# A feed-forward product as seven block products in place of eight, with its sums shared out anew over three engines

## The chip, the cores and the metric

The kernel runs on one core of one Trainium2 chip. A core has engines that run side by side, each through its own instructions in its own order: TensorE (PE in the profile; its weight loads are PEld), VectorE (DVE), ScalarE (ACT), GpSimd (POOL) and SyncE (SP, which here only issues transfers). TensorE writes only to PSUM, a memory of eight banks; VectorE and ScalarE read from there, and GpSimd works on SBUF alone in this kernel. The metric is device time in microseconds, as the median of a few executions.

## The reference

A block of a transformer on 4096 tokens of width 256, all in float32. With `xn = layernorm(x)`:

```
out = x + attn_block(xn) + experts(xn)

attn_block(xn):  x1 = layernorm(xn + attention(xn)) * gamma + beta
                 h  = gelu(x1 @ W1 + b1)            # W1: 256 x 1024
                 return x1 + h @ W2 + b2            # W2: 1024 x 256
experts(xn):     softmax over 8 experts, the best 2 of each token,
                 sum of share_k * expert_k(xn)      # hidden width 816
```

The change concerns the product `x1 @ W1` and what is added up around the feed-forward part: `x`, `x1`, `b2`, `h @ W2`, and for each token the two expert results with their shares.

## The kernel before

The kernel has three stages: normalization and routing; a long stage that interleaves the experts' products with attention, `STEPS = 32` steps and a few more; and at the end the feed-forward part. The change is in the last stage, which begins at about 850 us, and in a few lines that prepare it.

**The feed-forward stage** runs over `NG = 8` groups of `G = 512` tokens. A tile with 128 partitions holds 4 x 128 tokens (`TG = 4`) of width `D = 256`, or, turned, 2 x 128 features (`DC = 2`) by 512 tokens. For group g:

- `second_loads(g)` loads `x` into `acc` and the attention block's result into `x2`, both through SP's queue. `second_norm(g)` normalizes `x2` on ScalarE (line 1177), four instructions.
- `second_base(g)` puts `x + x1*gamma + beta + b2` into `acc` by three VectorE instructions of 128x1024 (lines 1188 to 1190).
- `turned2(g)` transposes `x2` on TensorE (line 1197) into two PSUM banks and ScalarE writes them to `x2T` with gamma and beta (line 1200).
- `hidden(g)` makes `hT`: for each of the `FC1 = 8` feature blocks f two matmuls with 512 moving columns into one bank (line 1210), then one GELU with its bias by ScalarE straight from the bank (line 1217).
- `sums_of_hidden(g)` makes four sums of `hT` quarters on VectorE (lines 1241 to 1245), which `second(g)` needs: the second product `h @ W2` is already done there in the form with seven block products in place of eight (Winograd's variant of Strassen's scheme). Its weight sums `V2` are made once by GpSimd in `sums_of_weights` (line 1235).
- `second(g)` has seven products p1, p2, p6, p5, p7, p3, p4, each eight matmuls of 128x128 into a bank of its own (line 1281). After each, VectorE adds the bank into `acc` (lines 1291, 1301, 1309). p1 is first copied by ScalarE to the tile `u` (line 1294).
- `picked(g)` gathers, by eight indirect transfers that GpSimd issues (line 1255), the two expert results of each token, and `combined(g)` adds them into `acc`, weighted with `share`, by eight VectorE instructions of 128x256 (line 1268).
- `store(g)` writes `acc` to the output through SP's queue.

**Order.** A manual schedule is in force: every engine gets its instructions in the order in which the code issues them, and none is moved before an earlier one of its own engine. The loop runs one group ahead with the hidden part: in turn g it issues `hidden(g)`, `second_base(g+1)`, `combined(g-1)`, `turned2(g+1)`, `second_norm(g+2)`, `picked(g)`, and then `second(g-1)` with the sums of `hidden(g)` between its products. So ScalarE's order in a turn is: eight GELUs, two copies of `turned2`, four of `second_norm`, the copy of `u`. VectorE's is: three of `second_base`, eight of `combined`, the adds of p1 and p2, two sums, p6 and p5, two sums, p7, p3, p4.

**Banks.** `bank()` hands out seven PSUM banks in rotation. A matmul that starts a bank waits until the reader of the use seven before is done.

Of the kernel before, what the change touches and what calls it, by code (L numbers as in the profile page):

```python
# [32 lines left out]
F32 = mybir.dt.float32  # L33
# [8 lines left out]
P = 128  # L42
# [61 lines left out]
def block_kernel(ctx: ExitStack, tc: tile.TileContext, a: dict, out: bass.AP):  # L104
# [1080 lines left out]
    def second_base(g, acc, x2):  # L1185

        scaled = accp.tile([P, TG, D], F32, tag="scaled", name=f"scaled{g}", bufs=1)
        nc.vector.tensor_tensor(acc, acc, bcast(beta_b2, TG, 1), ALU.add)
        nc.vector.tensor_tensor(scaled, x2, bcast(gamma, TG, 1), ALU.mult)
        nc.vector.tensor_tensor(acc, acc, scaled, ALU.add)  # L1190

    def turned2(g, x2):
        x2T = turns.tile([P, DC, G], F32, tag="x2T", name=f"x2T{g}")
# [8 lines left out]
            )  # L1202
        return x2T

    def hidden(g, x2T):
        hT = hf.tile([P, FC1, G], F32, tag="hf", name=f"hf{g}")
        for f in range(FC1):
            ph = bank(f"ph{g}_{f}")
            for c in range(DC):
                nc.tensor.matmul(  # L1210
                    ph,
                    W1[:, c, f * P : (f + 1) * P],
                    x2T[:, c, :],
                    start=(c == 0),
                    stop=(c == DC - 1),
                )
            nc.scalar.activation(hT[:, f, :], ph, AF.Gelu, bias=b1[:, f : f + 1])  # L1217
        return hT


# [27 lines left out]

    def picked(g):

        ys = []
        for i in range(g * TG, (g + 1) * TG):
            for k in range(2):
                y = got.tile([P, D], F32, tag="got", name=f"got{i}_{k}")
                nc.gpsimd.indirect_dma_start(  # L1255
                    out=y,
                    out_offset=None,
                    in_=done,
                    in_offset=bass.IndirectOffsetOnAxis(ap=slot[:, k, i : i + 1], axis=0),
                )  # L1260
                ys.append(y)
        return ys

    def combined(g, acc, ys):
        for n, y in enumerate(ys):
            t, k = n // 2, n % 2
            i = g * TG + t
            nc.vector.scalar_tensor_tensor(  # L1268
                acc[:, t, :], y, share[:, k, i : i + 1], acc[:, t, :], ALU.mult, ALU.add
            )  # L1270

    def second(g, acc, hT, v):

        t1, t2 = slice(0, 2), slice(2, 4)
        u = hf.tile([P, 2, P], F32, tag="u", name=f"u{g}")

        def product(n, left, right):
            pb = bank(f"s{g}_{n}").rearrange("p (t n) -> p t n", n=P)[:, 0:2]
            for t in range(2):
                for f in range(FH):  # L1280
                    nc.tensor.matmul(  # L1281
                        pb[:, t, :],
                        left[:, f, t * P : (t + 1) * P],
                        right[:, f, :],
                        start=(f == 0),
                        stop=(f == FH - 1),
                    )
            return pb

        def add(t, cols, pb):  # L1290
            nc.vector.tensor_tensor(acc[:, t, cols], pb, acc[:, t, cols], ALU.add)  # L1291

        p1 = product(1, hT[:, F_LO, 0:B], W2[:, F_LO, C1])
        nc.scalar.copy(u, p1)  # L1294
# [6 lines left out]
        nc.vector.tensor_tensor(u, p6, u, ALU.add)  # L1301
        add(t1, C2, u)
        yield
        p5 = product(5, v[:, 0], V2[:, 0])
        add(t1, C2, p5)
        add(t2, C2, p5)
        yield
        p7 = product(7, v[:, 2], V2[:, 2])
        nc.vector.tensor_tensor(u, p7, u, ALU.add)
        add(t2, C1, u)  # L1310
        add(t2, C2, u)
        yield
        p3 = product(3, v[:, 3], W2[:, F_HI, C2])
# [40 lines left out]
    for b in range(ALWAYS):  # L1354
# [56 lines left out]
        if b == STEPS:  # L1411
            att.close()
            wf = pool(ctx, "wf", right)
            accp = pool(ctx, "accp", right, bufs=4)
            V2 = wf.tile([P, 4, FC1 // 2, P], F32, tag="V2", name="V2")
            W1, W2 = matrix(wf, "W1", F1, DC), matrix(wf, "W2", D, FC1)
# [12 lines left out]
            x2s = {n: second_loads(n) for n in range(2)}  # L1429
        if b == STEPS + 1:  # L1430
            sums_of_weights()
            *_, r2 = rstd_of(mv2, root_of(mv2, NT, "b"), NT, "b")
            nc.vector.scalar_tensor_tensor(shift2, mv2[:, :, 0], -1.0, r2, ALU.mult, ALU.mult)
            nc.vector.tensor_tensor(beta_b2, beta, b2, ALU.add)
# [57 lines left out]


    x2Ts = {n: turned2(n, x2s[n][1]) for n in range(2)}

    for b in range(ALWAYS, BLOCKS):
        nc.gpsimd.memset(xs[b], 0.0)
# [15 lines left out]
    late_done.close()  # L1513
    experts_done.close()
    hf = pool(ctx, "hf", right, bufs=2)
    got = pool(ctx, "got", right, bufs=8)
    second_base(0, *x2s[0])
    last = None

# [4 lines left out]
    for g in range(NG):  # L1524
        if g + 2 < NG:
            x2s[g + 2] = second_loads(g + 2)
        hT = hidden(g, x2Ts.pop(g))
        if g + 1 < NG:
            second_base(g + 1, *x2s[g + 1])
        if g > 0:  # L1530
            acc = x2s.pop(g - 1)[0]
            combined(g - 1, acc, ys)
        if 0 < g < NG - 1:
            x2Ts[g + 1] = turned2(g + 1, x2s[g + 1][1])
        if g + 2 < NG:
# [104 lines left out]
```

## Time and profile before

| | |
|---|---|
| median of 3 runs | 1069.93 us (1069.36 to 1071.85) |
| the profiled execution's own time | 1071.19 us |
| its span | 1069.5 us |
| start of the feed-forward products in it | 850.7 us |
| one turn of the loop, groups 1 to 6 | 27.12 us |

Busy time in one turn (932.41 to 959.53 us): TensorE 27.12 us, VectorE 15.86 us, ScalarE 9.05 us, GpSimd 7.95 us; the granted TensorE clock is 1.00 there.

The profile is read as follows. A row of a group has the line, the engine, the operation, the tiles written and read, the shape and the number of instructions, and after the bar the busy time in us and the mean of one in ns. In the list in order of time, the first number is the start in us from the begin of the span, the second the duration, and brackets show how long the engine had been idle and what ended that. Each float32 matmul appears as two records. A matmul's end is modelled, so that the distance between starts, not the duration, is its cost in a row of matmuls.

### The profile page before, as it was taken

How to read it: one execution, taken by the hardware profiler on the slowest of the kernel's cores; microseconds unless marked ns; L12 is line 12 of the kernel's file. 1: busy time of each engine (PE TensorE's matmuls, PEld its weight loads, DVE VectorE, ACT ScalarE, POOL GpSimd, SP SyncE). 2: the span in 40 equal slices, each digit the busy share in tenths (PEclk: the TensorE clock that was granted, in tenths of full speed). 3: DMA queues.
4: the chain of work that ended last, by engine and by line, in shares of the span. 5: the costliest groups of instructions: out<-in, count | busy, mean ns of one | idle time of the engine just before them, and what ended most of it. 6: DMA issues, size and time to landing. Idle time of an engine off the chain costs nothing. (4 is left out here: it accounts for less than half of the span.)

```text
span 1069.5 us, 20380 instructions
## 1 busy us (share of the span) xinstructions
PE 1057.4 (99%) x7278; PEld 860.8 (80%) x7278; DVE 753.9 (70%) x1852; ACT 572.6 (54%) x1329; POOL 587.8 (55%) x706
## 2 busy tenths in 40 slices
PE   9998999999999999999999999999999999999998
PEld 6577887887888888888888888888887757777778
DVE  6666876886787687788888988888532455555546
ACT  4526556656657556756675666566455353333320
POOL 5417766676576666676877777767520053222220
PEclk9999999999999999999999999999999999999999
DMA  8225434445345344544544444345584343333111
GB/s 287 75 102 204 139 129 173 172 150 180 118 143 183 129 146 165 199 139 143 177 175 139 176 158 181 138 167 173 187 310 145 123 137 114 99 99 96 63 60 40
DMA packets 61047, 158.67 MB, mean 148 GB/s; under 512 B 6576, under 2 KB 46896, under 8 KB 56208
## 3 DMA queue, kind: packets, MB, share of 16 engines
q1 hardware_dynamic: 53632, 139.33, 37.4%
q0 software_dynamic: 6480, 17.70, 5.2%
q8 instruction: 59, 0.97, 0.4%
q10 hardware_dynamic: 832, 0.30, 0.1%
q14 instruction: 44, 0.36, 0.1%
HBM read 135.43 MB, written 21.89 MB: 147 GB/s over the span
## 5 line engine op out<-in xcount | busy, mean ns | idle before, releaser
L839 PE MATMUL gu<-xsT,wg 128*128 128x256 f32 (+1 forms) x1632 | 364.4, 370 | 0.0
L839 PEld LDWEIGHTS gu<-xsT,wg 128*128 128x128 f32 x1632 | 290.0, 191 | 46.5 <-DVE nm L1047 8.6
L1255 POOL DMA_INDIRECT got<-done,slot x64 | 64.6, 1010 | 177.0 <-DVE acc L1268 106.8
L847 ACT ACTIVATE gs<-gu,wg 128x256 f32<-128x256 f32 (+1 forms) x204 | 92.2, 452 | 120.4 <-PE gu L839 116.0
L1074 POOL TENSOR_TENSOR pr<-pr 128x256 f32<-128x256 f32 x128 | 114.2, 892 | 67.0 <-ACT pr L1062 67.0
L848 DVE SCALAR_TENSOR_TENSOR hT<-gu,wg,gs 128x256 f32<-128x256 f32 (+1 forms) x204 | 91.9, 461 | 78.7 <-ACT gs L847 77.8
L1075 POOL TENSOR_TENSOR pr<-pr,ident 128x256 f32<-128x256 f32 x128 | 132.8, 1037 | 10.0
L1062 ACT ACTIVATE pr<-pr,nm 128x256 f32<-128x256 f32 x256 | 126.8, 497 | 1.0 <-ACT xsT L831 0.6
L1210 PE MATMUL ph<-x2T,W 128*128 128x512 f32 x256 | 111.0, 592 | 0.0
L1217 ACT ACTIVATE hf<-ph,b 128x512 f32<-128x512 f32 x64 | 43.9, 687 | 121.8 <-PE ph L1210 55.3
L1047 DVE CUSTOM_DVE_ANT_0 pr<-ps,mask 128x256 f32<-128x256 f32 x256 | 90.7, 421 | 16.6 <-PE ps L1033 16.6
L880 ACT ACTIVATE hT<-hT 128x512 f32<-128x512 f32 (+2 forms) x179 | 84.9, 485 | 32.5 <-DVE hT L848 22.4
L814 POOL DMA_INDIRECT xs<-xnd,token x71 | 69.0, 972 | 50.5 <-DVE paired_tiles L781 33.1
L1210 PEld LDWEIGHTS ph<-x2T,W 128*128 128x128 f32 x256 | 48.2, 190 | 57.9 <-issue 54.5
L1092 DVE TENSOR_TENSOR pr<-pr,rec 128x1024 f32<-128x1024 f32 x32 | 39.2, 1226 | 41.9 <-POOL pr L1074 41.9
L1105 POOL TENSOR_TENSOR xd<-xd,same 128x256 f32<-128x256 f32 x32 | 19.7, 617 | 83.7 <-DVE same L1103 83.5
L1291 DVE TENSOR_TENSOR acc<-u,acc 128x256 f32<-128x256 f32 x32 | 12.9, 423 | 68.7 <-ACT u L1294 68.1
L929 POOL TENSOR_TENSOR ts<-wd 128x384 f32<-128x384 f32 x54 | 54.1, 1001 | 2.1
L1062 ACT ACT_TABLE_LOAD x31 | 39.8, 1283 | 19.9 <-DVE nm L1047 19.9
L973 ACT COPY y<-sh 128x512 f32<-128x512 f32 x27 | 15.8, 586 | 61.4 <-PE sh L952 61.4
L1062 ACT ACTIVATION_READ_ACCUMULATOR pr<-pr,nm 128x1 f32 x256 | 48.3, 189 | 0.0
L952 PE MATMUL pe<-wd,hT 128*128 128x128 f32 x324 | 44.9, 275 | 0.0
(252 smaller groups left out, 2112.1 us busy)
## 6 DMA issues: line engine op xcount, KB each, us to landing
wg<-in_gate_up SPq DMA_DIRECT2D x37, 1670.5 KB, 7.1
wd<-in_down SPq DMA_DIRECT2D x37, 896.0 KB, 4.8
done<-y SPq DMA_DIRECT2D x30, 256.0 KB, 2.1
x<-in_x SPq DMA_DIRECT2D x8, 512.0 KB, 5.5
xnd<-xn SPq DMA_DIRECT2D x8, 512.0 KB, 5.2
res<-xnd SPq DMA_DIRECT2D x16, 256.0 KB, 2.9
x1d<-res SPq DMA_DIRECT2D x16, 256.0 KB, 2.2
x<-x1d SPq DMA_DIRECT2D x8, 512.0 KB, 4.6
```

The costliest lines, as they stand in the source:

```text
L814: nc.gpsimd.indirect_dma_start(out=x[:, t, :], out_offset=None, in_=xnd, in_offset=bass.IndirectOffsetOnAxis(ap=token[:, i : i + 1], axis=0),)
L839: nc.tensor.matmul(pb[:, k, :], w[:, lo : lo + P], xT[:, c, :], start=(c == 0), stop=(c == DC - 1),)
L847: nc.scalar.activation(gs, pb[:, 0, :], AF.Identity, bias=w[:, gb : gb + 1])
L848: nc.vector.scalar_tensor_tensor(hT[:, f, :], pb[:, 1, :], w[:, ub : ub + 1], gs, ALU.add, ALU.mult)
L880: nc.scalar.activation(hT[on, lo:hi, :], hT[on, lo:hi, :], AF.Silu)
L929: nc.gpsimd.tensor_tensor(out_, left_, right_, ALU.subtract)
L1047: nc.vector.tensor_tensor_reduce(out=pr[:, hh, j, :], in0=ps[hh][:, j, :], in1=mask[:, kinds[j], :], scale=-1.0, scalar=-LOWEST, op0=ALU.a ...
L1062: nc.scalar.activation(pr[:, hh, j, :], pr[:, hh, j, :], AF.Exp, bias=nm[:, j, hh : hh + 1], scale=-1.0, accum_out=sums[:, j, hh : hh + 1],)
L1074: nc.gpsimd.tensor_tensor(first, first, second, ALU.add)
L1075: nc.gpsimd.tensor_tensor(second, second, bcast(ident, 2, 1), ALU.mult)
L1210: nc.tensor.matmul(ph, W1[:, c, f * P : (f + 1) * P], x2T[:, c, :], start=(c == 0), stop=(c == DC - 1),)
L1255: nc.gpsimd.indirect_dma_start(out=y, out_offset=None, in_=done, in_offset=bass.IndirectOffsetOnAxis(ap=slot[:, k, i : i + 1], axis=0),)
```

## The change

Seven things change, all but two within the feed-forward stage:

1. `hidden(g)` computes `x1 @ W1` in the seven-product form. The quarters are two feature halves of the input by two token halves (`B = 256`) on one side, and on the other side two input halves by the two feature blocks 2m and 2m+1. For each of four m there are seven matmuls of 256 moving columns into four banks, a ScalarE copy of p1 into a new tile `q`, five VectorE instructions that put the sums together in `hT`, and two GELUs that now read `hT` from SBUF.
2. The weight sums `V1` for it are made once on GpSimd, after those of `V2`.
3. `sums_of_inputs(g)`: four subtractions of 128x256 on GpSimd for each group, behind `turned2(g)`.
4. `second_base` moves from VectorE to GpSimd, as twelve instructions of 128x256 in place of three of 128x1024.
5. The weighting of the picked rows moves from VectorE to ScalarE: `weighted(g-1)` issues two instructions of 128x256 after the GELUs of each m. `combined` is left with two VectorE adds of 128x1024, issued later, just before `second(g-1)`.
6. `picked(g)` is issued right behind `hidden(g)`, ahead of `second_base(g+1)`, into two larger tiles in place of eight small ones.
7. In `second`, two pairs of adds become one wider add each.

```diff
     def second_base(g, acc, x2):
 ...
-        nc.vector.tensor_tensor(acc, acc, bcast(beta_b2, TG, 1), ALU.add)
-        nc.vector.tensor_tensor(scaled, x2, bcast(gamma, TG, 1), ALU.mult)
-        nc.vector.tensor_tensor(acc, acc, scaled, ALU.add)
+        for t in range(TG):
+            a_, s_ = acc[:, t, :], scaled[:, t, :]
+            nc.gpsimd.tensor_tensor(s_, x2[:, t, :], gamma, ALU.mult)
+            nc.gpsimd.tensor_tensor(a_, a_, beta_b2, ALU.add)
+            nc.gpsimd.tensor_tensor(a_, a_, s_, ALU.add)
 ...
+    def blocks_of_first():
+        return W1.rearrange("p c (m e q) -> p e c m q", e=2, q=P)
+
+    def sums_of_first_weights():
+        m = blocks_of_first()
+        a11, a12, a21, a22 = m[:, 0, 0], m[:, 0, 1], m[:, 1, 0], m[:, 1, 1]
+        s1, s2, s3, s4 = (V1[:, k] for k in range(4))
+        nc.gpsimd.tensor_tensor(s1, a21, a22, ALU.add)
+        for out_, left_, right_ in ((s2, s1, a11), (s3, a11, a21), (s4, a12, s2)):
+            nc.gpsimd.tensor_tensor(out_, left_, right_, ALU.subtract)
+
+    def sums_of_inputs(g, x2T):
+        ts = turns.tile([P, 4, B], F32, tag="x2s", name=f"x2s{g}")
+        b11, b12, b21, b22 = x2T[:, 0, 0:B], x2T[:, 0, B:], x2T[:, 1, 0:B], x2T[:, 1, B:]
+        t1, t2, t3, t4 = (ts[:, k] for k in range(4))
+        for out_, left_, right_ in ((t1, b12, b11), (t2, b22, t1), (t3, b22, b12), (t4, b21, t2)):
+            nc.gpsimd.tensor_tensor(out_, left_, right_, ALU.subtract)
+        return x2T, ts
+
+    def hidden(g, x2T, ts, others):
         hT = hf.tile([P, FC1, G], F32, tag="hf", name=f"hf{g}")
-        for f in range(FC1):
 ...
-            nc.scalar.activation(hT[:, f, :], ph, AF.Gelu, bias=b1[:, f : f + 1])
+        w = blocks_of_first()
+        for m in range(FC1 // 2):
+            banks = [halves(bank(f"ph{g}_{m}_{k}")) for k in range(4)]
+            p1, p6, p7, p5, p2, p4, p3 = (banks[k // 2][:, k % 2, :] for k in range(7))
+            for to, left_, right_ in (
+                (p1, w[:, 0, 0, m, :], x2T[:, 0, 0:B]),
+                (p6, V1[:, 1, m, :], ts[:, 1]),
+                (p7, V1[:, 2, m, :], ts[:, 2]),
+                (p5, V1[:, 0, m, :], ts[:, 0]),
+                (p2, w[:, 0, 1, m, :], x2T[:, 1, 0:B]),
+                (p4, w[:, 1, 1, m, :], ts[:, 3]),
+                (p3, V1[:, 3, m, :], x2T[:, 1, B:]),
+            ):
+                nc.tensor.matmul(to, left_, right_, start=True, stop=True)
+
+            q = hf.tile([P, 3, B], F32, tag="q", name=f"q{g}_{m}")
+            both = hT[:, 2 * m : 2 * m + 2, :]
+            nc.scalar.copy(q[:, 0], p1)
+            nc.vector.tensor_tensor(q[:, 1], p6, q[:, 0], ALU.add)
+            nc.vector.tensor_tensor(q[:, 2], p7, q[:, 1], ALU.add)
+            nc.vector.tensor_tensor(both[:, :, B:], q[:, 1:3], bcast(p5, 2, 1), ALU.add)
+            nc.vector.tensor_tensor(both[:, :, 0:B], banks[2], q[:, 0::2], ALU.add)
+            nc.vector.tensor_tensor(both[:, 0, B:], p3, both[:, 0, B:], ALU.add)
+            for f in range(2 * m, 2 * m + 2):
+                nc.scalar.activation(hT[:, f, :], hT[:, f, :], AF.Gelu, bias=b1[:, f : f + 1])
+            next(others, None)
         return hT
 ...
     def picked(g):
-        ys = []
-        for i in range(g * TG, (g + 1) * TG):
+        ys = got.tile([P, 2, TG, D], F32, tag="got", name=f"got{g}")
+        for t in range(TG):
 ...
-    def combined(g, acc, ys):
 ...
-            nc.vector.scalar_tensor_tensor(
-                acc[:, t, :], y, share[:, k, i : i + 1], acc[:, t, :], ALU.mult, ALU.add
-            )
+    def weighted(g, ys):
+        for t in range(TG):
+            for k in range(2):
+                i = g * TG + t
+                nc.scalar.activation(
+                    ys[:, k, t, :], ys[:, k, t, :], AF.Copy, scale=share[:, k, i : i + 1]
+                )
+            yield
+
+    def combined(acc, ys):
+        for k in range(2):
+            nc.vector.tensor_tensor(acc, acc, ys[:, k], ALU.add)
 ...
         p5 = product(5, v[:, 0], V2[:, 0])
-        add(t1, C2, p5)
-        add(t2, C2, p5)
+        right = acc.rearrange("p (k t) d -> p k t d", k=2)[:, :, :, C2]
+        nc.vector.tensor_tensor(right, right, bcast(p5, 2, 1), ALU.add)
 ...
-        add(t2, C1, u)
-        add(t2, C2, u)
+        low = acc[:, t2, :].rearrange("p t (h n) -> p t h n", h=2)
+        nc.vector.tensor_tensor(low, low, bcast(u, 2, 2), ALU.add)
 ...
         if b == STEPS + 1:
             sums_of_weights()
+            sums_of_first_weights()
 ...
     x2Ts = {n: turned2(n, x2s[n][1]) for n in range(2)}
+    x2Ts = {n: sums_of_inputs(n, x2T) for n, x2T in x2Ts.items()}
 ...
-    got = pool(ctx, "got", right, bufs=8)
+    got = pool(ctx, "got", right, bufs=2)
 ...
     for g in range(NG):
 ...
-        hT = hidden(g, x2Ts.pop(g))
+        hT = hidden(g, *x2Ts.pop(g), weighted(g - 1, ys) if g > 0 else iter(()))
+        ys_last = ys if g > 0 else None
+        ys = picked(g)
         if g + 1 < NG:
             second_base(g + 1, *x2s[g + 1])
-        if g > 0:
-            acc = x2s.pop(g - 1)[0]
-            combined(g - 1, acc, ys)
         if 0 < g < NG - 1:
-            x2Ts[g + 1] = turned2(g + 1, x2s[g + 1][1])
+            x2Ts[g + 1] = sums_of_inputs(g + 1, turned2(g + 1, x2s[g + 1][1]))
         if g + 2 < NG:
             second_norm(g + 2, x2s[g + 2][1])
-        ys = picked(g)
+        acc = x2s.pop(g - 1)[0] if g > 0 else None
+        if g > 0:
+            combined(acc, ys_last)
         outs = second(g - 1, acc, *last) if g > 0 else iter(())
 ...
     acc = x2s.pop(NG - 1)[0]
-    combined(NG - 1, acc, ys)
+    list(weighted(NG - 1, ys))
     outs = second(NG - 1, acc, *last)
-    some(outs, 6)
+    some(outs, 2)
+    combined(acc, ys)
+    some(outs, 4)
```

More of the change, by code (lines that the diff above doesn't have):

```diff
@@ L1203, in turned2 @@
         return x2T
-    def hidden(g, x2T):
-        hT = hf.tile([P, FC1, G], F32, tag="hf", name=f"hf{g}")
-        for f in range(FC1):
[L1208 to L1215, printed above, removed]
-                )
-            nc.scalar.activation(hT[:, f, :], ph, AF.Gelu, bias=b1[:, f : f + 1])
+    def blocks_of_first():
+        return W1.rearrange("p c (m e q) -> p e c m q", e=2, q=P)
@@ L1249, in picked @@
     def picked(g):
-        ys = []
-        for i in range(g * TG, (g + 1) * TG):
+        ys = got.tile([P, 2, TG, D], F32, tag="got", name=f"got{g}")
+        for t in range(TG):
+            i = g * TG + t
             for k in range(2):
-                y = got.tile([P, D], F32, tag="got", name=f"got{i}_{k}")
                 nc.gpsimd.indirect_dma_start(
-                    out=y,
+                    out=ys[:, k, t, :],
                     out_offset=None,
@@ L1260, in picked @@
                 )
-                ys.append(y)
         return ys
-    def combined(g, acc, ys):
-        for n, y in enumerate(ys):
-            t, k = n // 2, n % 2
-            i = g * TG + t
-            nc.vector.scalar_tensor_tensor(
-                acc[:, t, :], y, share[:, k, i : i + 1], acc[:, t, :], ALU.mult, ALU.add
-            )
+    def weighted(g, ys):
+        for t in range(TG):
+            for k in range(2):
+                i = g * TG + t
+                nc.scalar.activation(
[5 more added lines that the diff above has]
+            nc.vector.tensor_tensor(acc, acc, ys[:, k], ALU.add)
     def second(g, acc, hT, v):
@@ L1415, in block_kernel @@
             V2 = wf.tile([P, 4, FC1 // 2, P], F32, tag="V2", name="V2")
+            V1 = wf.tile([P, 4, FC1 // 2, P], F32, tag="V1", name="V1")
             W1, W2 = matrix(wf, "W1", F1, DC), matrix(wf, "W2", D, FC1)
```

## The prediction

> **What bounds the kernel now.** I read the chain that ended last first, then one turn of the feed-forward loop in order of time, engine by engine. The chain, in order of time, one turn:
>
> ```profile
> 918.68 13.74 PE ph L1210 x32
> 932.41 0.87 PE pt L1197 x8
> 933.29 12.51 PE s L1281 x112
> 945.79 13.73 PE ph L1210 x32
> ```
>
> TensorE alone, without a gap: 13.74 + 0.87 + 12.51 = 27.12 us a turn. All other engines are covered. The same turn on VectorE and ScalarE shows how their queues behave:
>
> ```profile
> 932.45 0.69 ACT L1217 ACTIVATE hf<-ph,b 128x512 f32<-128x512 f32 x1 [1.03 <-PE ph L1210]
> 933.04 1.44 ACT L1200 ACTIVATE x2T<-pt,beta_c,gamma_c 128x512 f32<-128x512 f32 x2
> 934.36 2.07 ACT L1177 ACTIVATE x<-x,shift,r_b 128x256 f32<-128x256 f32 x4
> 936.33 0.36 ACT L1294 COPY u<-s 128x256 f32<-128x256 f32 x1
> 936.72 0.43 DVE L1291 TENSOR_TENSOR acc<-u,acc 128x256 f32<-128x256 f32 x1 [10.38 <-ACT u L1294]
> 937.59 1.22 DVE L1241 TENSOR_TENSOR hv<-hf 128x1024 f32<-128x1024 f32 x1
> 939.98 0.42 DVE L1301 TENSOR_TENSOR u<-s,u 128x256 f32<-128x256 f32 x1
> 940.43 0.43 DVE L1291 TENSOR_TENSOR acc<-u,acc 128x256 f32<-128x256 f32 x1
> ```
>
> To see here: the last GELU ended at 933.14, so line 1241 could have run then. It ran at 937.59, behind an add that waited 10.38 us for ScalarE's copy of `u`. Each engine keeps its written order, and a wait holds everything behind it. Today this costs nothing, since TensorE does not need the result soon.
>
> **The change, part by part.**
>
> *TensorE.* Eight records of 128x256 (line 839, from 500.62 to 502.35 us) take 1.73 us, so a matmul with its two records is 0.433 us. The new hidden part has 4 x 7 of them: 12.13 us against 13.74, a gain of 1.61 us a group, 12.9 us in eight. If TensorE stayed the bound, that would be all.
>
> *The new round trip.* For each m the order is: ScalarE copies p1; VectorE does five instructions on it; ScalarE does two GELUs on their result, then two weighting instructions; and only behind these stands ScalarE's copy for m+1, on which VectorE's five for m+1 wait. Before, a GELU needed only TensorE. Now the two engines hand one m back and forth and neither can start the next. The rows:
>
> ```profile
> L1160 DVE TENSOR_TENSOR res<-wo,res 128x512 f32<-128x512 f32 x16 | 11.0, 689 | 0.7 <-PE wo L1157 0.7
> L1294 ACT COPY u<-s 128x256 f32<-128x256 f32 x8 | 2.9, 363 | 13.9 <-PE s L1281 13.9
> L880 ACT ACTIVATE hT<-hT 128x512 f32<-128x512 f32 x93 | 58.6, 631 | 19.2 <-DVE hT L848 18.2
> L1177 ACT ACTIVATE x<-x,shift,r_b 128x256 f32<-128x256 f32 x32 | 16.5, 599 | 0.0
> ```
>
> - copy of p1: 0.36, with the hand-over 0.40.
> - VectorE: three of 128x256 at 0.42 and two of 128x512 with one PSUM operand at 0.69: 2.64; dependent ones add 0.03 (939.98 to 940.43), independent ones overlap as much. 2.65.
> - two GELUs: from PSUM they step at 0.58 (the first two take 1.27 together); from SBUF there is no such row, so between 0.58 and 0.73 (631 of SiLU and some 0.1 for the bias). I take 0.64: 1.28.
> - two weightings: no row of this function; four of line 1177 with two per-partition operands step at 0.5 (2.07 us), with one operand less I take 0.42, the ends being 0.36 and 0.5. 0.84.
> - two hand-overs: 0.03.
>
> Together 5.2 us for each m, against 3.03 us that TensorE needs for its seven matmuls.
>
> *A whole turn.* From the moment VectorE is free for m = 0: its five, 2.65; three round trips, 15.6; then ScalarE must get from the last five to the copy of `u`: GELUs and weightings 2.12, `turned2` 1.40, `second_norm` 2.0, copy 0.36, hand-over 0.05: 5.9. The two adds of `combined` (2 x 1.22) fit in there. Then VectorE's tail behind `u`: 936.72 to 946.25, 9.5 us, less 0.4 that it waited for TensorE and 0.1 for the merged adds: 9.0. Sum 2.65 + 15.6 + 5.9 + 9.0 = 33.2. Group g's five for m = 0 stand behind that tail, so the turns do not overlap: this is the period, and TensorE waits for banks in it. It was 27.12.
>
> *GpSimd.* A turn has eight gathers at 1.25 (10.0), and 16 instructions of 128x256 at 0.61 (line 1105, 617 ns): 19.8 us, below either period. `second_base` runs beside VectorE's five, `picked` moves past it without holding it up. The base is wanted a turn later. The four subtractions start after `turned2`, together with `combined` and the sums of `hidden`. These have two SBUF inputs, and this is where an engine's gain is paid by another:
>
> ```profile
> L938 DVE TENSOR_TENSOR ss<-hT 128x384 f32<-128x384 f32 x27 | 15.0, 554 | 0.0
> L940 DVE TENSOR_TENSOR hT<-hT 128x384 f32<-128x384 f32 x27 | 29.2, 1081 | 0.0
> ```
>
> The same shape takes 554 ns alone and 1081 (967 and 891 on lines 939 and 962) beside GpSimd's line 929: 0.41 more on average. By that row four subtractions cost VectorE at most 4 x 0.41 = 1.6 us. The Trainium skill, "SBUF — State Buffer", the section on the two sides of SBUF, says the port pair that GpSimd shares with a VectorE instruction of two SBUF inputs is locked for a whole instruction: 4 x 0.61 = 2.4 us. Half of it falls on `combined`, which has slack. I take 0.8: the period is 34.0 us.
>
> *Once-only work.* The four sums for `V1`, 4 x 1.27 = 5.1 us (line 1235), follow `V2`'s, which end at 791.4; `sums_of_inputs` for groups 0 and 1 run from 811.5 (end of `turned2`) to 816.4, and push the clearing of `xs` from 794.8 to about 816.4 to 818.3. Its first VectorE writer is at 828.9, a store of a cleared tile at 817.8: hidden, at most 0.5 us on SP's queue. There the next loads stand behind `store`, some 7 us later a turn; `second_norm` wants them over 20 us later.
>
> *The sum*, from 850.7 us. Group 0 has no weighting and no `second`: m = 0 waits for TensorE (3.7), the GELU table load 1.28, three round trips of 4.36 (13.1), GELUs 1.35, four sums 4.9: 24.3. Groups 1 to 5: 5 x 34.0 = 170. Group 6 has no `second_norm`, group 7 no `turned2` either; there `combined` (done 4.6 after the last five) replaces the 5.9: 2 x 32.7 = 65.4. VectorE is then at 259.7. The last `second` is again TensorE's: its 13 remaining products of 1.787 us run from about 243 and end at 266.3, with the last add 266.8. The end is 850.7 + 266.8 + 3.2 (1069.5 less 1066.3, the store) = 1120.7 us against the span of 1069.5: +51.2. The profiled execution took 1071.2, 1.3 above the median; the same +51.2 on the median gives **1121 us**.
>
> *The clock.* A longer wait of TensorE could bring its clock down:
>
> ```profile
> 86.88 0.55 PE L827 MATMUL pts<-ident,xs 128*128 128x128 f32 x3 [2.92 <-DMA xs<-xnd,token]
> ```
>
> Behind it, by stretches of 1 us:
>
> ```profile
> 87.00:88.00 1.00, 1.00 (x7) 0.92 (x8) 0.94 (x1) 0.48 (x1) 0.92 (x2) 1.00 0.97 395
> 88.00:89.00 1.00, 1.00 (x5) 0.79 (x4) 0.38 (x2) 0.10 (x1) 1.00 (x2) 0.56 0.93 391
> ```
>
> After 2.92 us of idling the granted clock (third from the right) was 0.50 for some 3.2 us. My longest wait in a turn is 2.5 us, where `hidden` wants the bank of p6; the others are 1.5 or less, and from 835 to 842 us waits of 0.6 left it at 1.00. One such drop costs TensorE 1.6 us, within its slack. "TensorE: Matmul & The Clock Gate" of the skill, in the section on the second failure mode, speaks against this: short idling between groups of matmuls that cycle through PSUM banks makes the clock swing to half. By that, with all waits cold, seven matmuls take 6.1 us, more than the 5.2; a turn would be 2 x 25.5 = 51 us and the span up to 1260. I follow the row and keep part of this for the range.
>
> **Rivals.**
>
> *TensorE stays the bound.* The gain of 12.9 us comes whole: 1057. A turn takes 17.5 + 0.8 + 3 x L, with L the round trip; it equals 27.1 at L = 2.9. Below that the change is faster. For it speaks that all engines' work fits (VectorE: 15.9 less 3.7 and 1.3, and 10.6 more: 21.5 of 25.5). Against it is the order that line 1291 shows. L without any weighting is still 4.4. Chance 0.04.
>
> *The weighting is hidden after all*, or VectorE's five overlap more: L = 4.4, a turn 31.6, and the end 1121 - 7 x 2.4 = 1104, with shorter hand-overs 1096. Chance 0.10.
>
> *The clock falls in every turn.* Two drops of 1.6 us that reach the path in each turn: 1121 + 7 x 3.2 = 1143; always cold, 1260. Chance 0.13.
>
> *Nothing to measure.* The measurement tells 0.2%, 2 us; only a round trip that eats exactly the gain ends there. Chance 0.01.
>
> **How the numbers follow.** The round trip has 0.72: 1121. The low end is the hidden weighting; the high end takes slow GELUs and weightings (0.73 and 0.5: 0.34 x 3 + 0.34 a turn, +10 us), the full lock (2.4 in place of 0.8 a turn, +11), and a first part of the clock: 1148. Between 1096 and 1148 I see 8 in 10. Faster 0.05 (the first rival and a little for what I overlook), same 0.01, slower 0.94.
>
> **What would show it.** A turn of 33 to 35 us; TensorE's hidden matmuls at 0.433 us but with waits between them; ScalarE's copy to `q` following the weighting at once, and VectorE's first add of each m waiting about 2.5 us for it; VectorE busy some 22 us a turn; sums on lines 1241 to 1245 above 1.22 us where GpSimd subtracts. A clock of 1.00. I am wrong if copies for m+1 start before the GELUs of m, if VectorE's fives follow each other at 3 us, or if the clock reads 0.5 to 0.8 over the stage.

## The result, and the profile after

The changed kernel takes **1115.65 us** (median of 4 runs, 1114.58 to 1117.32) against 1070.49 us of the kernel before in the same comparison: 1.042 times as long, with a 95% interval from 1.0403 to 1.0437. That is 45 us more; the forecast was 51 more. The profiled execution has a span of 1115.6 us. Line numbers below are those of the kernel that the row belongs to.

The list in order of time, changed kernel, ScalarE and VectorE over one block m of a group (start, duration, instruction, and in brackets how long the engine had stood idle and for what):

```profile
948.91 0.42 DVE L1250 TENSOR_TENSOR q<-ph,q 128x256 f32<-128x256 f32 x1 [2.45 <-ACT q L1249]
...
951.11 0.42 DVE L1254 TENSOR_TENSOR hf<-ph,hf 128x256 f32<-128x256 f32 x1
951.56 1.33 ACT L1256 ACTIVATE hf<-hf,b 128x512 f32<-128x512 f32 x2 [2.68 <-DVE hf L1254]
952.80 0.89 ACT L1307 ACTIVATE got<-got,share 128x256 f32<-128x256 f32 x2
953.60 0.35 ACT L1249 COPY q<-ph 128x256 f32<-128x256 f32 x1
953.98 0.42 DVE L1250 TENSOR_TENSOR q<-ph,q 128x256 f32<-128x256 f32 x1 [2.45 <-ACT q L1249]
```

VectorE stands idle 2.45 us until ScalarE has copied p1; ScalarE stands idle 2.68 us until VectorE has made the block. Each waits for the other in turn, and one lap takes 953.98 - 948.91 = 5.07 us. The two groups of instructions, summed over the whole run (busy time, mean ns, idle time before):

```profile
L1256 ACT ACTIVATE hf<-hf,b 128x512 f32<-128x512 f32 x64 | 42.7, 714 | 114.7 <-DVE hf L1254 114.7
L1250 DVE TENSOR_TENSOR q<-ph,q 128x256 f32<-128x256 f32 x32 | 13.5, 422 | 58.6 <-ACT q L1249 58.6
```

One turn of the loop in the table by stretches (stretch, its length, busy time and number of records of PE, PEld, DVE, ACT and POOL, granted clock, DMA share, GB/s), first before:

```profile
932.41:959.53 27.12, 27.12 (x155) 19.42 (x153) 15.86 (x26) 9.05 (x15) 7.95 (x8) 1.00 0.32 97
```

and after:

```profile
938.70:971.20 32.50, 27.28 (x177) 23.51 (x176) 21.32 (x35) 13.22 (x27) 20.91 (x25) 1.00 0.26 81
```

Before, TensorE was busy for all of its turn. After, no engine is: the bound is the order in which two of them wait for each other. The clock stays at 1.00. The chain that ended last, which was TensorE's 27.12 us a turn, is in the changed kernel VectorE's alone, from 1091.80 us to the last store's issue at 1111.49; three of its pieces:

```profile
1097.27 1.14 DVE hv L1281
...
1103.89 0.69 DVE acc L1355
...
1107.47 1.22 DVE acc L1314
```

The longest wait of TensorE in the stage comes at its start, between groups 0 and 1 (list in order of time, VectorE and TensorE):

```profile
872.36 1.80 DVE L1281 TENSOR_TENSOR hv<-hf 128x1024 f32<-128x1024 f32 x1 [1.46 <-ACT hf L1256]
874.20 1.63 DVE L1282 TENSOR_TENSOR hv<-hv,hf 128x1024 f32<-128x1024 f32 x1
875.75 1.74 DVE L1284 TENSOR_TENSOR hv<-hf 128x1024 f32<-128x1024 f32 x1
877.42 1.21 DVE L1285 TENSOR_TENSOR hv<-hf,hv 128x1024 f32<-128x1024 f32 x1
878.55 0.41 DVE L1250 TENSOR_TENSOR q<-ph,q 128x256 f32<-128x256 f32 x1
879.02 1.22 PE L1245 MATMUL ph<-x2T,V 128*128 128x256 f32 x2 [6.08 <-DVE q L1250]
```

VectorE's four sums of group 0's hidden units, for which nobody waits yet, stand ahead of its first instruction on group 1. Line 1250 frees the bank that TensorE wants. The sums themselves are longer than their usual 1.22 us, beside GpSimd's base. The granted clock (third from the right) over three stretches of 1 us there:

```profile
874.00:875.00 1.00, 0.00 (x0) 0.00 (x0) 0.96 (x2) 0.50 (x2) 0.92 (x2) 1.00 0.37 95
...
876.00:877.00 1.00, 0.00 (x0) 0.00 (x0) 1.00 (x1) 0.00 (x0) 0.85 (x2) 0.50 1.09 386
...
882.00:883.00 1.00, 1.00 (x4) 0.81 (x3) 0.00 (x0) 1.00 (x3) 0.69 (x2) 0.50 0.28 74
```

### The profile page after: what moved, and what is told of

Same layout as the page of the kernel before. It is cut to its first block, busy times and chain, and to the rows that moved or that the text cites. A ratio compares the mean times of both kernels' runs of the same rounds, so it can differ in the third digit from the quotient of the medians.

```text
span 1115.6 us, 21145 instructions
## 1 busy us (share of the span) xinstructions
PE 1060.4 (95%) x7470; PEld 896.0 (80%) x7470; DVE 798.5 (72%) x1924; ACT 605.1 (54%) x1425; POOL 694.1 (62%) x838
## 5 line engine op out<-in xcount | busy, mean ns | idle before, releaser
L1256 ACT ACTIVATE hf<-hf,b 128x512 f32<-128x512 f32 x64 | 42.7, 714 | 114.7 <-DVE hf L1254 114.7
L880 ACT ACTIVATE hT<-hT 128x512 f32<-128x512 f32 (+2 forms) x179 | 84.9, 485 | 32.5 <-DVE hT L848 22.4
L1295 POOL DMA_INDIRECT got<-done,slot x64 | 67.6, 1056 | 46.3 <-issue 45.4
L1250 DVE TENSOR_TENSOR q<-ph,q 128x256 f32<-128x256 f32 x32 | 13.5, 422 | 58.6 <-ACT q L1249 58.6
L1245 PE MATMUL ph<-x2T,W 128*128 128x256 f32 x128 | 40.4, 398 | 15.2 <-DVE u L1353 9.7
L1226 POOL TENSOR_TENSOR x2s<-x2T 128x256 f32<-128x256 f32 x16 | 12.0, 751 | 61.6 <-ACT x2T L1202 61.6
L1245 PE MATMUL ph<-x2s,V 128*128 128x256 f32 x192 | 49.2, 390 | 0.0
```

The costliest lines, as they stand in the source:

```text
L880: nc.scalar.activation(hT[on, lo:hi, :], hT[on, lo:hi, :], AF.Silu)
L1245: nc.tensor.matmul(to, left_, right_, start=True, stop=True)
L1295: nc.gpsimd.indirect_dma_start(out=ys[:, k, t, :], out_offset=None, in_=done, in_offset=bass.IndirectOffsetOnAxis(ap=slot[:, k, i : i + 1] ...
```

## The experiments

Two theories stood against each other. **Round trip**: the copy of p1 for m+1 stands in ScalarE's queue behind GELUs and weightings of m, which wait for VectorE's five sums of m, and so ties the two engines. **Rival**: some other part makes it slower, such as GpSimd's new work and its effect on VectorE, TensorE itself, or the total of VectorE's work. The diffs are against the changed kernel unless said otherwise. All comparisons in brackets are with the kernel before, run beside it, with the 95% interval.

**1. The copy first.** The copy of p1 for m+1 is issued ahead of GELUs and weightings of m, which `finish(m)` now holds. Nothing else differs.

```
             nc.scalar.copy(q[:, 0], p1)
+            if m > 0:
+                finish(m - 1)
 ...
-            for f in range(2 * m, 2 * m + 2):
-                nc.scalar.activation(hT[:, f, :], hT[:, f, :], AF.Gelu, bias=b1[:, f : f + 1])
-            next(others, None)
+        finish(FC1 // 2 - 1)
```

> The whole change, with one thing moved: ScalarE's copy of p1 for block m+1 stands ahead of the GELUs and weightings of m. Round-trip theory: VectorE's fives no longer wait for ScalarE's GELUs and follow at TensorE's pace of 3.03 us; a turn is about 2.5 + 3 x 3.0 + 5.6 + 8.8 = 26 us, at most 28.5 with waits for banks, where the change has 32.5; the time falls by 35 to 48 us to 1068 to 1081 us. Rival, that the engines are simply fuller (VectorE 21.3 us and GpSimd 20.9 us busy a turn, and the port that they share): no more than 10 us are won, 1105 or above, as no work is taken away.

Measured: 1081.76 us (1.0108, 1.0091 to 1.0125). This is just above what the round trip's theory gave (1068 to 1081); the rival asked for 1105 or more. The single move takes back 34 of the 45 us. Turns are now 33.4, 25.5, 26.0, 27.8 and 30.1 us (distances of the transposes on line 1199): the best are where TensorE alone would put them, the rest vary. By this trace it is GpSimd that lengthens them (list in order of time, this kernel):

```profile
971.70 3.15 DVE L1320 TENSOR_TENSOR acc<-acc,got 128x1024 f32<-128x1024 f32 x2 [1.86 <-POOL acc L1191]
972.05 1.71 POOL L1190 TENSOR_TENSOR scaled<-x,gamma 128x256 f32<-128x256 f32 x1
973.73 1.71 POOL L1191 TENSOR_TENSOR acc<-acc,beta_b 128x256 f32<-128x256 f32 x1
975.52 0.73 POOL L1192 TENSOR_TENSOR acc<-acc,scaled 128x256 f32<-128x256 f32 x1
...
983.84 1.13 PE L1251 MATMUL ph<-x2s,V 128*128 128x256 f32 x4 [0.96 <-POOL x2s L1226]
```

GpSimd's instruction takes 0.73 us alone and 1.71 while a VectorE sum of two SBUF inputs runs beside it. It falls behind, and TensorE waits for its input sums, 9.8 us in five waits. That this is what lengthens the turns is tested in experiment 6.

**2. The weighting on VectorE again**, as it was before; everything else stays.

```
-    def combined(acc, ys):
-        for k in range(2):
-            nc.vector.tensor_tensor(acc, acc, ys[:, k], ALU.add)
+    def combined(g, acc, ys):
+        for t in range(TG):
+            for k in range(2):
+                i = g * TG + t
+                nc.vector.scalar_tensor_tensor(
+                    acc[:, t, :], ys[:, k, t, :], share[:, k, i : i + 1], acc[:, t, :], ALU.mult, ALU.add
+                )
 ...
-        hT = hidden(g, *x2Ts.pop(g), weighted(g - 1, ys) if g > 0 else iter(()))
+        hT = hidden(g, *x2Ts.pop(g), iter(()))
```

> The change with its weighting of the picked rows put back on VectorE (eight instructions of 128x256 in combined), nothing else. Round-trip theory: the weightings stand in ScalarE's queue between the GELUs of m and the copy for m+1, so without them a round trip is 5.06 - 0.80 = 4.26 us and a turn 32.5 - 4 x 0.8 = 29.3 us; combined's 3.75 us fit beside ScalarE's 4.9 us; about 22 us less, 1093 us. Rival, that VectorE's load is the bound: 1.3 us more a turn, 1125 us.

Measured: 1096.93 us (1.0247, 1.0230 to 1.0264). In the table by stretches one turn reads

```profile
949.23:978.79 29.56, 27.20 (x177) 23.54 (x177) 23.49 (x42) 10.04 (x19) 19.92 (x25) 1.00 0.29 90
```

VectorE has 2.2 us more to do and the turn is 2.97 us shorter. Work was added to the busier of the two engines, and the kernel became 19 us faster: the lap of a block is 4.27 us here, 0.80 less, since the weighting has left it. The forecast was 1093, so some 4 us of the gain are missing. A total of VectorE's work as the bound is ruled out.

**3. Eight products again**, with the rest of the change kept: GpSimd's base, ScalarE's weighting, merged adds.

> The change with hidden in its old form (eight block products, GELU straight from PSUM, no sums for it on GpSimd or VectorE), all else of the change kept: second_base on GpSimd, weighting on ScalarE behind every second GELU, picked ahead. Round-trip theory: the round trip is gone, TensorE is the bound with 27.1 us a turn, 1070 us within 3. Rival, that the sharing out costs by itself (GpSimd's port lock, ScalarE's weightings ahead of its other work): above 1080 us.

Measured: 1071.89 us (1.0004, 0.9997 to 1.0010). The diff puts the former `hidden` back in place of the new one, with `next(others, None)` after every second GELU, and leaves out `V1` and the input sums. One turn:

```profile
930.00:957.12 27.12, 27.12 (x154) 19.43 (x153) 13.32 (x15) 12.22 (x24) 23.88 (x23) 1.00 0.32 101
```

Sharing out the sums costs nothing by itself: VectorE has 2.5 us less, GpSimd 15.9 more, and TensorE does not notice. The whole loss belongs to the seven products as they are ordered here.

**4. p1 computed twice**, so that TensorE does eight matmuls a block again within the same round trip.

```
                 (p1, w[:, 0, 0, m, :], x2T[:, 0, 0:B]),
+                (p1, w[:, 0, 0, m, :], x2T[:, 0, 0:B]),
```

> The change with the first of the seven matmuls of each block issued twice into the same bank, so that TensorE has again eight matmuls a block, 4 x 0.433 = 1.73 us more a turn. Round-trip theory: TensorE waits some 5 us a turn, the additional work goes into these waits, the time stays at 1115 us, at most 4 us above it. Rival, that TensorE is still on the path: 8 x 1.73 = 14 us more, 1129 us.

Measured: 1113.93 us (1.0409, 1.0392 to 1.0427). One turn, with TensorE busy for 28.81 us in place of 27.28:

```profile
938.70:971.20 32.50, 28.81 (x186) 25.11 (x185) 21.30 (x36) 13.22 (x27) 20.93 (x25) 1.00 0.26 81
```

The turn is 32.50 us as in the change. TensorE's work is off the path: what the change saves there was worth nothing.

**5. The seven products alone**, put into the kernel before, with `V1` and the input sums, which they need, but base and weighting left on VectorE (diff against the kernel before: `hidden`, `sums_of_first_weights`, `sums_of_inputs` of the change and their calls).

> The kernel before with only the seven-product form of hidden, its weight sums and its input sums; second_base and the weighting stay on VectorE, picked and second as before. Round-trip theory: a round trip of 4.26 us, then second_base and combined (3.66 + 3.75) on VectorE ahead of its tail of 9.0: 2.5 + 12.8 + 7.4 + 9.0 = 31.7 us a turn, 1105 to 1116 us, as slow as the whole change. Rival, that the sharing out of the sums is what costs: 1060 to 1075 us.

Measured: 1120.8 us (1.0452, 1.0434 to 1.0470): slower than the whole change. That is above the 1105 to 1116 of the round trip's theory, and far from the rival's 1060 to 1075. One turn:

```profile
948.20:981.37 33.17, 29.34 (x185) 25.29 (x184) 27.15 (x46) 10.04 (x20) 12.52 (x12) 0.99 0.27 80
```

The lap is 4.27 us here (no weighting in it), 0.8 less than in the change, but the turn is longer: between two groups ScalarE now stands idle 10.2 us for VectorE (7.2 in the change), which has its base and weighted sums there. So, by experiments 3 and 5 together, the sharing-out of the sums does no harm and with the seven products even helps, by 3 to 5 us (by ratio and by median).

What remained was why the better order did not reach the 1057 us at which TensorE alone would end. The following kernels all build on experiment 1.

**6. GpSimd's base of group 1 ahead of the loop**, in time that GpSimd has idle.

```
     second_base(0, *x2s[0])
+    second_base(1, *x2s[1])
 ...
-        if g + 1 < NG:
+        if 0 < g < NG - 1:
             second_base(g + 1, *x2s[g + 1])
```

> The copy moved ahead as in the first experiment, and second_base for group 1 issued on GpSimd before the loop, ahead of picked(0), where GpSimd had idled some 27 us. GpSimd theory for what the first experiment left (1081.8 against 1060): GpSimd starts the loop behind by some 9 us and never gets that back, its subtractions come late and TensorE waits for them (9.8 us in five waits); with the base out of the way at the start these waits go and the time falls by 5 to 10 us to 1072 to 1077. Rival, that the 3.95 us wait of TensorE in group 1 and the half clock behind it are what was left: no change, 1080 to 1082.

Measured: 1071.06 us against 1072.92 (0.9977, 0.9966 to 0.9989). The gain is somewhat above the 5 to 10 us that were expected. GpSimd's lateness was the loss of experiment 1: every turn from the first transpose on is 25.47 us (887.75, 913.22, 938.69 and so on), which is TensorE's work without a gap and 1.65 less than 27.12. But the first transpose comes late (882.91 us in experiment 1), behind a wait in group 1. The move has also brought the gathers of groups 0 and 1 together: GpSimd now issues 16 in a row, which matters in what follows.

```profile
878.14 1.22 PE L1251 MATMUL ph<-x2T,V 128*128 128x256 f32 x2 [5.94 <-DVE q L1258]
```

**7. The sums of group 0 moved, too.** VectorE's four sums of group 0's hidden units (lines 1281 to 1285 of the changed kernel) go behind group 1's sums of the products, and `second_norm` goes behind the copy of `u`.

```
         hT = hidden(g, *x2Ts.pop(g), weighted(g - 1, ys) if g > 0 else iter(()))
+        if g == 1:
+            last = hT_first, next(sums)
+            some(sums, 1)
 ...
-        if g + 2 < NG:
-            second_norm(g + 2, x2s[g + 2][1])
 ...
         some(outs, 2)
+        if g + 2 < NG:
+            second_norm(g + 2, x2s[g + 2][1])
```

> As the last, and two more moves in the order alone: the four sums of hidden(0) stand on VectorE behind the fives of group 1 in place of ahead of them, and second_norm stands behind the copy of u on ScalarE. If VectorE's sums in group 0 made TensorE's wait of 3.95 us there and the half clock that followed, both go: 5 to 6 us less than the last. second_norm later brings u 2 us earlier to VectorE, which matters only if VectorE is the bound in a turn: 0 to 10 us less. Together 1060 to 1070; by the theory that GpSimd is the bound alone, no more than 3 us less than the last.

Measured: 1072.44 us (0.9995, 0.9986 to 1.0005): **missed**; only the number of the other theory, no more than 3 us less than experiment 6, came. First transpose 886.98 us, no better than 887.75. VectorE's sums were out of the way and TensorE waited 4.98 us at nearly the same place, for another reason (list in order of time):

```profile
863.41 0.59 PE L1251 MATMUL ph<-x2T,V 128*128 128x256 f32 x2
869.97 0.42 DVE L1262 TENSOR_TENSOR hf<-ph,hf 128x256 f32<-128x256 f32 x1 [1.41 <-PE ph L1251]
873.92 0.95 POOL L1301 DMA_INDIRECT got<-done,slot  x1 [0.30 <-issue]
875.67 0.37 ACT L1255 COPY q<-ph 128x256 f32<-128x256 f32 x1 [1.95 <-remote]
876.08 0.42 DVE L1258 TENSOR_TENSOR q<-ph,q 128x256 f32<-128x256 f32 x1 [5.69 <-issue]
876.56 1.22 PE L1251 MATMUL ph<-x2T,V 128*128 128x256 f32 x2 [4.98 <-issue]
```

TensorE's p3 of the last block has its rows at 863.41. VectorE's instruction that waits for it begins at 869.97, 6.6 us later; usually it is 1.1. In the brackets, "issue" and "remote" are waits for which the profile names no releaser among the engines. TensorE, VectorE and ScalarE all go on within 2 us of the end of the last of 16 gathers, which GpSimd had issued in a row from 855.11 to 874.87.

**8. One of four token tiles of the base on VectorE**, to relieve GpSimd, in the version of experiment 7. `rest(lo, hi, engine)` holds the base's three instructions for the token tiles from `lo` on.

```
+        rest(0, TG - 1, nc.gpsimd)
+        return lambda: rest(TG - 1, TG, nc.vector)
```

> As the last, with one token tile of four of second_base on VectorE, in the gap where it waits for the weightings ahead of combined (1.9 us; the three instructions take 1.3). GpSimd then has 21.6 - 2.2 = 19.4 us of unlocked work a turn. If GpSimd with the port's locks is the bound, turns that grew to 28 and 30 us in the first experiment stay at 25.5: 1058 to 1063, below the kernel before. If VectorE is the bound, it has 1.3 us more a turn: 5 to 10 us above the last.

Measured: 1074.93 us (1.0022, 1.0010 to 1.0034), 2.5 above the one before: missed by both. The turns were 25.47 us already and stayed so, so that there was nothing to gain. The 2.5 us are lost at the start (second transposes at 916.54 in place of 914.03 us): base 1 needs the buffer `scaled`, which VectorE now uses for group 0's last token tile, and GpSimd stood idle for 28.96 us, until 853.69, ahead of it. The gathers so began at 860.91 in place of 855.11 and ended at 880.72. The stop moved with them: one of VectorE's sums of products waited here until the last gather was done.

```profile
880.76 0.69 DVE L1265 TENSOR_TENSOR hf<-ph,q 128x512 f32<-128x512 f32 x1 [6.34 <-remote]
```

**9 and 10. The gathers of group 1 later**, behind base and input sums of group 2; 9 in the version of experiment 7, 10 in that of experiment 6.

```
+        if g != 1:
             ys = picked(g)
 ...
         x2Ts[g + 1] = sums_of_inputs(g + 1, turned2(g + 1, x2s[g + 1][1]))
+        if g == 1:
+            ys = picked(g)
```

> The version with all three reorderings, with one thing moved: on GpSimd the eight gathers of the picked rows of group 1 stand behind the base and the input sums of group 2, in place of directly behind the eight gathers of group 0. Between 861 and 876 us of the version before it, ScalarE and VectorE saw TensorE's products of group 0 and group 1 later and later after the times at which the trace has them (0.3 us, then 2, 5 and 12 us), while the 16 gathers were issued back to back from 855 to 875. Theory that the gathers (or what they share with TensorE's messages) hold these up: the lag shrinks once only eight stand there, the stage's start gains 4 to 9 us, 1064 to 1068 us. Rival, that the lag belongs to the stage's start itself (the loads at full DMA share, the clock, the order copy, GELU): it stays, 1070 to 1074 us.

> The same move of the eight gathers of group 1 alone, made in the version with the copy first and the base of group 1 early (sums of hidden units of group 0 still ahead of the five sums of group 1). Gathers as the cause: the lag of TensorE's products goes, but VectorE's four sums (6.4 us) still stand ahead of group 1's first five, so part of the loss stays: 1066 to 1070 us against 1071. Rival (start itself): 1070 to 1073 us.

Measured: 1075.90 us (1.0016, 1.0009 to 1.0024) and 1077.47 us (1.0039, 1.0026 to 1.0053); against 1074.06. Both missed what the gathers' theory said; 9 is just above what the rival gave, 10 above both. The trace of 9 shows why the time says so little. The first transpose came at 882.87 us, 4.1 earlier. Then the loss stood one turn later, where the moved gathers met those of group 2 and again made 16 in a row, from 893.24 to 913.62:

```profile
903.86 0.59 PE L1251 MATMUL ph<-x2T,W 128*128 128x256 f32 x2
...
909.94 0.37 ACT L1255 COPY q<-ph 128x256 f32<-128x256 f32 x1 [3.38 <-PE ph L1251]
912.67 0.95 POOL L1301 DMA_INDIRECT got<-done,slot  x1 [0.30 <-issue]
915.55 0.42 DVE L1259 TENSOR_TENSOR q<-ph,q 128x256 f32<-128x256 f32 x1 [4.79 <-remote]
916.45 0.37 ACT L1255 COPY q<-ph 128x256 f32<-128x256 f32 x1 [4.12 <-remote]
916.80 1.94 PE L1199 MATMUL pt<-ident,x 128*128 128x128 f32 x8 [5.28 <-remote]
```

The copy at 909.94 is that of the p1 with its rows at 903.86: 6.1 us. The next turn was 33.9 us, then 27.4, then 25.47. Kernel 10 has the same picture (gathers 891 to 912, waits for "remote" of 2.67, 4.51 and 7.60 us).

**11. The gathers apart**: those of group 1 between base and input sums of group 2, so that nowhere two groups of eight meet (diff against experiment 7: the two hunks above, the second one line higher).

> The version with all three reorderings, with the eight gathers of group 1 moved on GpSimd behind the base of group 2 but ahead of the input sums of group 2, so that nowhere two groups of eight gathers stand one behind the other without other work between them. In the two versions in which they had been moved behind the input sums, the stage's start gained 4.1 us and the lost time came back at 904 to 917 us, where again 16 gathers stood back to back (893 to 914) and every engine went on within 4 us of the last one. Theory that 16 gathers in a row hold up TensorE's messages: both losses go, turns of 25.5 us from the second transpose on, 1064 to 1068 us. Rival (the loss belongs to loads that fill the DMA engines, or to something else that is only pushed along): 1070 to 1076 us again, with a late turn somewhere in the first three.

Measured: 1071.38 us (1.0011, 0.9999 to 1.0022), by its time again the rival's. In the trace the delays are gone: the same p3 has its rows at 862.67 and its reader begins at 863.80, and the first transpose is at **876.00** us, 11 us earlier. Nine of the 11 are then lost in five turns of 27.5 us on average. Waits of TensorE for GpSimd over the stage (us in total, times, longest), and one of these turns:

```profile
PE ph L1251 <- POOL x2s L1226: 8.2, 8, 1.9
...
929.46:957.58 28.12, 26.00 (x178) 23.83 (x176) 24.21 (x37) 14.59 (x30) 25.43 (x25) 1.00 0.32 99
```

GpSimd is busy for 25.4 us of this turn (22.5 of 25.47 in experiment 7). With the 0.30 us that stand ahead of each of its eight gathers it has next to no time left: it is the bound now, with several of its base and input sums at 1.6 to 1.7 us beside VectorE's.

**12. The gathers apart, and one tile of the base on VectorE**: experiments 11 and 8 together.

> The version before this one (gathers of groups 0 and 1 apart) began its turns 11.0 us earlier than the one with all three reorderings (third group's transposes at 876.0 against 887.0 us), and lost 9 of them again in five turns of 27.5 us on average in place of 25.5, in which TensorE waits for GpSimd's input sums. Here one of the four token tiles of the base (three of GpSimd's twelve sums and products a group, 2.2 us or more) goes to VectorE, as was done once already where the start still cost its 11 us. Theory that the start and GpSimd's share are the two remaining losses: turns of 25.5 us from 876 on, 10 us less than 1071.4, so 1060 to 1064 us. Rival, that the gain of the start only lasts while something else is late (VectorE, then at some 25 us a turn, or the gathers back to back again): 1068 to 1075 us.

Measured: **1065.63 us** (1063.70 to 1067.27) against 1072.30, a ratio of 0.9933 (0.9920 to 0.9946): faster than the kernel before, and 4.5% below the changed one. It is just above what the first theory gave, and below the rival's. Turns from the transposes: 28.6 and 26.2 us, then 25.47 to the end, in which TensorE is busy without a gap:

```profile
934.43:959.90 25.47, 25.47 (x177) 23.97 (x176) 23.96 (x40) 13.95 (x29) 20.87 (x23) 1.00 0.34 105
```

The first transpose is at 879.62, 3.6 later than in 11, for the reason of experiment 8 (GpSimd idle 28.96 us for `scaled`, so that the gathers begin at 862.36). TensorE's waits for GpSimd are 0.7 us in all.

## Why the prediction was right

The sign, the mechanism and the time (inside 1096 to 1148, 5 us under the likeliest) came out. That it came so near is in part luck: some of its terms were off, one way and the other. By its steps:

- **The lap**, 5.2 us: measured 5.07. Two GELUs from SBUF step 1.24 (I took 1.28), two weightings 0.80 (0.84), the copy with its hand-over 0.38 (0.40); the five sums with theirs are 2.65, as taken. Without weighting the lap is 4.27 (4.36). Experiment 1 shows it as the cause; experiments 2 to 5 leave the other explanations no room.
- **The turn**, 34.0 us: measured 32.5. Three laps are 0.4 shorter, ScalarE's way to the copy of `u` 0.2. The rest is contention with GpSimd, for which I took 0.8. In the turn shown above, the first add of `u` took 0.56 in place of 0.42, and that is all of it that stood on the path: `combined` took 2.90 in place of 2.44, but it had slack, and the four sums on lines 1281 to 1285 stayed at 1.22 us, as GpSimd's subtractions were all but done. So the 0.8 was too much, and the 2.4 us a turn that I estimated from the rule of the Trainium skill's "SBUF — State Buffer", the section on the two sides of SBUF, far too much. The rule itself does fit where the two engines meet: VectorE's 1.22 us sums on lines 1281 to 1284 took 1.63 to 1.80 beside GpSimd's base, and GpSimd's 0.73 us became 1.71 in experiment 1, so that each was held for most of an instruction of the other.
- **The rows for that contention** were misread. In the kernel before, GpSimd's instructions beside lines 939, 940 and 962 are those of lines 1074 and 1075, not 929, and line 938 is not alone in any of its 27 cases (list in order of time, kernel before):

```profile
536.62 0.56 DVE L938 TENSOR_TENSOR ss<-hT 128x384 f32<-128x384 f32 x1
536.83 0.93 POOL L1074 TENSOR_TENSOR pr<-pr 128x256 f32<-128x256 f32 x1 [1.77 <-ACT pr L1062]
...
537.84 0.93 POOL L1075 TENSOR_TENSOR pr<-pr,ident 128x256 f32<-128x256 f32 x1
538.10 1.08 DVE L940 TENSOR_TENSOR hT<-hT 128x384 f32<-128x384 f32 x1
```

  Line 938 began first and kept its 0.55 us; GpSimd's instruction, begun 0.21 us later, took 0.93 in place of 0.73. At line 940 GpSimd was first, and VectorE took 1.08. So what the rows show is that the one that starts later pays, not that VectorE pays each time.
- **The sum**: the stage began 2.0 us later, from a wait for a gather near 86 us that ended 1.2 us later, and a longer stretch at half clock behind it, in a part where the two kernels' work is the same. Group 0 took 1.5 us more, most of it in its four sums (6.2 us in place of 4.9, beside GpSimd's base). The turns of groups 1 to 6, counted by VectorE's first sum of each, were 7.2 us shorter together. Group 7 and the end were 1.4 shorter; there VectorE and not TensorE finished last, which the sum had the other way round. 1120.7 + 2.0 + 1.5 - 7.2 - 1.4 = 1115.6, as measured.
- **GpSimd**, 16 x 0.61: **wrong row**. Line 1105 reads an operand that is repeated along the free axis; with two full operands the same shape costs 0.73 us (step 0.68 to 0.81). Busy 20.9 us a turn is still below the turn, so that it cost nothing here. It would have mattered to the first rival: in experiments 1 and 11 GpSimd is what keeps TensorE from its gain.
- **"My longest wait in a turn is 2.5 us"**: wrong at the start, where it was 6.08. The sum of times had group 0's four sums ahead of group 1's first block, but I read TensorE's waits from the steady turn alone. The clock was at 0.50 for some 10 us there, from 875.1 to 885.3; TensorE had slack, so that VectorE's turn for group 1 (32.8 us) hardly shows it. In the steady turns the waits are 0.6 to 1.6 us and the clock stays 1.00; the swing that the skill's "TensorE: Matmul & The Clock Gate", second failure mode, describes did not come with waits of that length.
- **The rivals**: "TensorE stays the bound" needed a lap of 2.9 us. No lap got that short in the order of the change. With the copy first (experiment 1 and 6 to 12) there is no lap any more, since the copy does not wait for the block before it, and in the turns that nothing else delayed TensorE did become the bound, at 25.47 us as worked out (27.12 - 1.61 = 25.51).

**Left open.** What makes the other engines see TensorE's products late near the gathers is not settled. Delays came in all five stretches of 16 gathers in a row (experiments 6 to 10), and in the last four of them the engines went on within 4 us of the last gather, also where the stretch had been moved by 6 us (8) or by more than 35 (9 and 10). With eight in a row the delays were absent in experiment 11 and about 2 us in experiment 9, whose instructions are the same up to that place. Loads filled the DMA engines (a share of about 1.0) in part of each such stretch, but also beside the eight gathers of 11, so that neither loads nor gathers alone have been shown to do it. These versions also vary more from run to run (1068.95 to 1075.55 for 11) than the kernel before does (1069.59 to 1072.19 beside it); whether for the same reason is not shown.

## What to carry to other kernels

When a result goes from one engine to another and back, look in the queue of each for what stands ahead of the hand-over: a short copy behind a long dependent instruction can make a bound of two engines that are both idle for much of the time, and moving that one copy ahead of it gave back three quarters of the loss. Check the start of a stage apart from its steady turn, since its first instructions stand behind work that nobody needs yet. And when one bound is removed, work out the next engine's turn with the durations that it has beside its neighbours (here GpSimd's 1.7 us, not 0.73), and try to spread a burst of transfers that one engine issues in a row: here the start came up to 11 us earlier, though the reason is open.

## What the runs showed of the hardware

The same 24 instructions of GpSimd kept it busy for 22.5 us a turn or 25.5, according to when they met VectorE's (experiments 7 and 11: from 964.96 us on in the one and 957.58 in the other, four and six of its base and input sums took about 1.6 us or more). The time at which the two engines meet thus sets GpSimd's speed, and a version that starts earlier can have slower turns. And TensorE's rows can stand 6.6 us (experiment 7) ahead of the moment at which VectorE sees the product, where the usual distance is 1.1 us: at such a place the release times of the waiting engines say more than TensorE's own rows.
